# Ending a Strassen-style FFN kernel in two halves of its tokens: the last group's second layer, its norms and its stores

## The chip, the core and the metric

The kernel runs on one core of a Trainium2 chip. The metric is the device time of one execution in microseconds. PE is TensorE (matrix products), DVE is VectorE, ACT is ScalarE, POOL is GpSimd, SP is SyncE, which here only issues DMAs. PSUM is the memory that PE writes to, in banks of 128 partitions by 512 float32 values; SBUF is the working memory.

## The reference

Input x is 4 batches of 512 tokens of 256 features, float32. First a gated scan with its projections, then a feed-forward stack of six blocks, each wrapped in a LayerNorm and a residual:

```python
x = x + _layernorm(_L0_attn_ref(_layernorm(x), ...))
x = x + _layernorm(_L0_ffn_ref(_layernorm(x), ...))

def _L0_ffn_ref(x, W1, B1, W2, B2, LN_G, LN_B):      # N_BLOCKS 6, DIM 256, HIDDEN 1024
    for i in range(N_BLOCKS):
        h = jax.nn.gelu(jnp.einsum('bsd,hd->bsh', x, W1[i]) + B1[i], approximate=False)
        x = jnp.einsum('bsh,dh->bsd', h, W2[i]) + B2[i] + x
        if i < N_BLOCKS - 1:
            x = _layernorm(x, LN_G[i], LN_B[i])
    return x
```

The change concerns the very end: the second product of block 5 for the last two batches, the LayerNorm behind it, the sum with x and the store of the result.

## The kernel before, in words

The four batches form two groups of two (`g` = 0, 1; a group has 1024 tokens). In the feed-forward stack the features lie on the partitions. Both products of a block are done with fewer block products and more sums (a fast matrix multiplication). The first layer (`Hidden`, fed step by step with `take`) makes 1024 hidden features in four `Row`s of 256. `Row.got` applies gelu on ACT and then makes four sums t1 to t4 of hidden blocks: t1 and t3 on DVE (for one row on POOL), t2 and t4 on POOL. These are the tiles `tc`. The second layer (`Output`) has seven parts `p1` to `p7` of four products each, one per row; `p6`, `p5`, `p7`, `p4` read the sums. `partial` takes a PSUM bank, adds the bias and the block's input (DVE, `scalar_tensor_tensor`), `total`, `total11` and `p3` add a second bank (DVE, `tensor_tensor`). Index d is the half of the features, n the batch within the group.

For the last group of the last block, `Output` splits only parts `p5` and `p3` into two columns of 256 tokens; the other five run over 512. Then `finish(u)` does two tiles of 128 tokens: four transposes on PE bring them to a bank with tokens on the partitions, `token_stats` (two DVE instructions per tile) gives mean and variance, `rstd_of` on POOL makes in four small instructions eps added (`ve`), the power −1/2 (`r`), minus the mean (`nm`) and their product (`nb`). ACT adds `nb` to the tile of x, DVE multiplies the bank by `r` and adds, SP issues the store. Two calls follow each half of `p3`: first the tiles of n = 0, then those of n = 1. Other groups have another path through DRAM (`norm`), which ends for the last block in four POOL adds `n<-n,room` and four stores per batch.

The order of instructions on each engine is not that of the program text. `Plan.op` collects every operation with an engine, a cost and its dependencies; `Plan.latest` gives each a due time, counting back from the end of PE's work, and `Plan.run` lets each engine take the one due first of those that are ready by the plan's own costs. An operation that nobody reads (a store) gets as its due time the place that the backward walk over PE has reached (`last[n] = at`).

The end of the program and the line with the due time:

```python
            elif last[n] == 1e9:
                last[n] = at
```

Of the kernel before, what the change touches and what calls it, by code (L numbers as in the profile page):

```python
# [13 lines left out]
ALU = mybir.AluOpType  # L14
PSUM = bass.MemoryType.PSUM

P = 128
LN_EPS = 1e-5
SIGN = {"+": ALU.add, "-": ALU.subtract}
RMS_EPS = 1e-6  # L20
ORDER = "p1 p2 p6 p7 p4 p5 p3".split()
DEFER = 7
HEAD, BY = 2, (2, 1)
POOLROWS = (2,)
WARM = 6
FILL = 2

# [225 lines left out]
class Plan:  # L253
# [31 lines left out]
    def latest(self):  # L285

        last = [1e9] * len(self.ops)
        at = sum(cost for engine, cost, *_ in self.ops if engine == "PE")
        for n in reversed(range(len(self.ops))):
            engine, cost, _, deps, _ = self.ops[n]  # L290
            if engine == "PE":
                at = min(at - cost, last[n])
                last[n] = at
            elif last[n] == 1e9:
                last[n] = at
            for d in deps:
# [51 lines left out]
def kernel(  # L348
# [210 lines left out]
            dst.size * P * 4 / 0.26e6,  # L559
        )  # L560

    def store(dst, src):
        kept = isinstance(dst, View)
        to = dst.ap if kept else dst
        plan.op(
            "SP",
            0.45,
            lambda: nc.sync.dma_start(out=to, in_=src.ap),
            [src],
            [dst] if kept else [],  # L570
            src.size * P * 4 / 0.26e6,
        )
# [461 lines left out]
    class Output:  # L1034


        def __init__(self, i, g, hidden):
            self.i, self.hidden = i, hidden

            n = 2 if (i, g) == (NB - 1, NG - 1) else 1  # L1040
            self.parts = [ts(k, S // n) for k in range(n)]
            w = w2_s
            self.x = xts[g]
            self.left = [(part[:2], int(j)) for part in ORDER for j in part[3:] or "0123"]
            if n == 2:
                half = NP // 2
                self.left = [("p1", j) for j in range(NP)] + [("p2", j) for j in range(NP)]
                self.left += [("p6", j) for j in range(NP)] + [("p5", j) for j in range(half)]
                self.left += [("p7", j) for j in range(NP)]
                self.left += [("p5", j) for j in range(half, NP)] + [("total11", 0)]  # L1050
                self.left += [("p4", j) for j in range(NP)]
# [4 lines left out]
            self.sf, self.s11 = [[None] * 2 for _ in range(ND)], None  # L1056

        def take(self, count=1):
            for part, j in self.left[:count]:
                getattr(self, part)(j)  # L1060
            del self.left[:count]

        def partial(self, d, n):
            s = wide.next()
            stt(s, self.px, b2_s[:, self.i, d : d + 1], self.x[d][n], ALU.add, ALU.add)
            return s

        def total(self, d, n, bank, s):
# [3 lines left out]
        def used(self, j):  # L1072

            self.uses[j] = self.uses.get(j, 0) + 1
            if self.uses[j] == 2:
                hts.back(self.hidden.rows[j].grids[0])

        def done(self, d, n, s):

            self.sf[d][n] = [s[:, ts(t, P)] for t in range(NT)]  # L1080
            if len(self.parts) > 1:
                return
            if n not in self.sent:
                self.sent[n] = rooms.next(), passed.next()
            block, there = self.sent[n]

            part = block[:, ts(d, S)]
            part = part.with_ap(part.ap.rearrange("p (g t r) -> p g t r", g=Q, t=NT))
            blocks_transposed(part, s.ap.rearrange("p (t g c) -> p g t c", t=NT, g=Q), s)
            wide.back(s)  # L1090
            store(there[:, ts(d, S)], block[:, ts(d, S)])
            if all(self.sf[k][n] for k in range(ND)):
                to = self.tokens[n] = rooms.next()
                collected(there, to)
                rooms.back(block)

        def p1(self, j):
            if j == 0:
                self.px = banks.next()
            product(self.px, self.a11[j], self.hidden.rows[j].h[0][0], j == 0)  # L1100
            self.used(j)
            if j == NP - 1:
                self.sn1 = self.partial(0, 0)

        def p2(self, j):
            if j == 0:
                self.py = banks.next()
            product(self.py, self.a12[j], self.hidden.rows[j].h[1][0], j == 0)
            self.used(j)
            if j == NP - 1:  # L1110
                self.total(0, 0, self.py, self.sn1)
                banks.back(self.py)

        def p6(self, j):
            product(self.px, sb2[1][:, j, :], self.hidden.rows[j].sums[1], False)
            tcs.back(self.hidden.rows[j].sums[1])
            if j == NP - 1:
                self.sn2 = self.partial(0, 1)

        def p5(self, j):  # L1120
            if j == 0:
                self.pz = [banks.next()[:, cols] for cols in self.parts]
            for pz, cols in zip(self.pz, self.parts):
                t1 = self.hidden.rows[j].sums[0]
                product(pz, sb2[0][:, j, :], t1[:, cols], j == 0)
            tcs.back(self.hidden.rows[j].sums[0])
            if j == NP - 1 and len(self.parts) == 1 and self.s11:
                self.total11()

        def p7(self, j):  # L1130
            product(self.px, sb2[2][:, j, :], self.hidden.rows[j].sums[2], False)
            if j == NP - 1:
                self.s11 = self.partial(1, 1)
                if len(self.parts) == 1 and " ".join(ORDER).rindex("p5") < " ".join(ORDER).rindex("p7"):
                    self.total11()

        def total11(self, _=None):
            s = self.s11
            for pz, cols in zip(self.pz, self.parts):
                tt("DVE", s[:, cols], pz, s[:, cols], ALU.add)  # L1140
            self.done(1, 1, s)

        def p4(self, j):
            product(self.px, self.a22[j], self.hidden.rows[j].sums[3], False)
            tcs.back(self.hidden.rows[j].sums[3])
            if j == NP - 1:
                s = self.partial(1, 0)
                banks.back(self.px)
# [1 line left out]

        def p3(self, j, part=0):
            pz, cols = self.pz[part], self.parts[part]
            b22 = self.hidden.rows[j].h[1][1]
            product(pz, sb2[3][:, j, :], b22[:, cols], False)
            if part == len(self.parts) - 1:
                hts.back(self.hidden.rows[j].grids[1])
            if j == NP - 1:
                s = wide.next()[:, cols]
                tt("DVE", s, pz, self.sn2[:, cols], ALU.add)
                if len(self.parts) == 1:  # L1160
                    self.done(0, 1, s)
                else:
                    self.sf[0][1] = self.sf[0][1] or []
                    self.sf[0][1] += [s[:, ts(k, P)] for k in range(s.size // P)]
                banks.back(pz)
                if part == len(self.parts) - 1:
                    wide.back(self.sn2)

    class Norm:

# [131 lines left out]
    for i in range(NB):  # L1302
        for g in range(NG):
# [26 lines left out]
            hidden.take(26)  # L1330
            if g == 1 and i + 1 < NB:
                w1_sums(i + 1)
            output = Output(i, g, hidden)
            for u in range(4):
                output.take(2)
                norm.features(u)
            output.take(len(output.left) - DEFER)
            of = (i, g)
    output.take(len(output.left))
    norm = Norm(*of, output)  # L1340
    norm.load_x(0)
    norm.load_x(1)
    for part in range(2):
        for j in range(NP):
            output.p3(j, part)
        norm.finish(2 * part)
        norm.finish(2 * part + 1)
    plan.run()


# [45 lines left out]
```

## Time and profile before

| what | us |
|---|---|
| median of three runs (686.39 to 688.34) | 686.4 |
| the profiled execution | 687.01 |
| its span, from the first to the last instruction | 685.2 |
| PE busy in the span | 671.6 |
| POOL busy in the span | 529.1 |
| DVE busy in the span | 469.2 |
| ACT busy in the span | 358.0 |
| PE's granted clock, mean over the span | 0.996 of full speed |

The times come from one profiled execution; the time of a run is measured around it. In rows of groups, the form `out<-in` names what an instruction writes and reads, then come partitions by elements, the count, the busy time and the mean duration in ns. In the timeline a row has start, duration, engine, line, and what ended the engine's idle time before it. PE rows count two matrix passes for every float32 product, and PEld is the load of its weights, which overlaps other passes. Rows with a q (SPq) are the queue's: they issue DMAs. Nearly all operations are recorded in helpers, so their lines are those of the helper (L502 `tt`, L514 `tscalar`, L524 `stt`, L485 and L487 `act`, L534 `product`, L545 `transpose`, L568 `store`), and groups are told apart by tile names.

### The profile page before, as it was taken

Reading aid. Unit: us, or ns where it says so; the run is one execution under the profiler, and the core shown is the slowest. Engines: PE = TensorE matmul, PEld = TensorE weight load, DVE = VectorE, ACT = ScalarE, POOL = GpSimd, SP = SyncE. Lnnn points to the kernel's source line nnn. Section 1 sums busy time; section 2 is a strip of 40 time slices with the busy share of each in tenths; the row PEclk is TensorE's granted clock in tenths of the full one; section 3 lists DMA queues with packets and bytes.
Section 4 is the critical chain, followed back from the end, with each engine's and each line's share of the span. In section 5 each row is a group of like instructions: output and inputs, shape, how many; then the busy total and the mean of one; then the engine's idle time right before and its main releaser. Section 6 shows DMA issues by size and latency. Waiting matters only on the chain.

```text
span 685.2 us, 8143 instructions
## 1 busy us (share of the span) xinstructions
PE 671.6 (98%) x2328; PEld 436.1 (64%) x2328; DVE 469.2 (68%) x897; ACT 358.0 (52%) x625; POOL 529.1 (77%) x688
## 2 busy tenths in 40 slices
PE   8999999999999999999999999999999999999994
PEld 6565568747658568477476585684774765856853
DVE  5567666866938839759569388397595694783955
ACT  3847757725734636437257346364472573463722
POOL 4997769858988668996589886689965898865763
PEclk9999999999999999999999999999999999999998
DMA  8401312143262142440432622414404206226411
GB/s 254 163 1 62 122 62 80 45 154 92 92 200 77 63 153 53 172 159 17 153 94 73 219 77 76 139 40 178 161 23 154 92 2 225 81 70 190 130 42 63
DMA packets 81837, 73.73 MB, mean 108 GB/s; under 512 B 6272, under 2 KB 70784, under 8 KB 81792
## 3 DMA queue, kind: packets, MB, share of 16 engines
q1 hardware_dynamic: 80960, 72.29, 32.7%
q10 hardware_dynamic: 832, 0.92, 0.4%
q8 instruction: 19, 0.31, 0.2%
q14 instruction: 26, 0.21, 0.1%
HBM read 43.82 MB, written 29.36 MB: 107 GB/s over the span
## 4 chain that ended last, share of the span: by engine, by line
PE 64%; DVE 16%; POOL 8%; ACT 4%; issue 3%; DMA 2%; SPq 0%; DVEq 0%; ACTq 0%; POOLq 0%
PE bank L534 60%; DVE ht L502 9%; POOL tc L502 5%; PE pt L534 4%; DVE tmp L502 2%; DVE st L671 2%; ACT ht L485 2%; DVE tc L502 1%; POOL tx L502 1%; POOL r L502 1%; ACT tmp L487 1%; DMA passed<-room 1%; DMA xt<-in_wk 1%; DVE mv L672 1%; POOL r L514 1%
## 5 line engine op out<-in xcount | busy, mean ns | idle before, releaser
L534 PE MATMUL bank<-tx,sa 128*128 128x256 f32 x672 | 163.1, 381 | 1.7 <-ACT tmp L487 1.5
L487 ACT COPY tmp<-bank 128x512 f32<-128x512 f32 x144 | 83.8, 583 | 137.0 <-PE bank L534 128.2
L534 PEld LDWEIGHTS bank<-tx,sa 128*128 128x128 f32 x672 | 126.4, 190 | 28.3 <-issue 8.2
L502 POOL TENSOR_TENSOR tc<-ht,tc 128x512 f32<-128x512 f32 x96 | 123.6, 1299 | 24.4 <-ACT bank L485 20.6
L485 ACT ACTIVATE ht<-ht,b 128x512 f32<-128x512 f32 x156 | 106.9, 715 | 12.5 <-DVE ht L502 12.5
L502 DVE TENSOR_TENSOR ht<-tmp,bank 128x512 f32<-128x512 f32 x156 | 101.2, 679 | 17.7 <-ACT tmp L487 12.8
L534 PE MATMUL bank<-tc,w 128*128 128x512 f32 x208 | 95.1, 594 | 0.0
L502 DVE TENSOR_TENSOR tmp<-tmp,bank 128x512 f32<-128x512 f32 x96 | 64.4, 677 | 40.2 <-PE bank L534 23.3
L534 PE MATMUL bank<-tc,sb 128*128 128x512 f32 (+1 forms) x200 | 88.2, 581 | 0.9
L534 PE MATMUL bank<-ht,sb 128*128 128x512 f32 (+1 forms) x200 | 88.2, 576 | 0.0
L524 DVE SCALAR_TENSOR_TENSOR tmp<-bank,b,xt 128x512 f32<-128x512 f32 x48 | 35.5, 740 | 76.2 <-PE bank L534 76.2
L534 PE MATMUL bank<-ht,w 128*128 128x512 f32 x192 | 84.4, 593 | 0.0
L502 POOL TENSOR_TENSOR tx<-xt,tx 128x256 f32<-128x256 f32 x108 | 75.8, 734 | 1.0
L485 ACT ACTIVATE n<-x,r 128x256 f32<-128x256 f32 x96 | 50.4, 581 | 37.4 <-POOL r L502 37.4
L534 PEld LDWEIGHTS bank<-tc,sb 128*128 128x128 f32 x200 | 37.2, 190 | 49.6 <-issue 37.9
L534 PEld LDWEIGHTS bank<-tc,w 128*128 128x128 f32 x208 | 39.3, 190 | 40.9 <-issue 37.5
L502 POOL TENSOR_TENSOR tx<-xt 128x256 f32<-128x256 f32 x24 | 17.5, 727 | 60.1 <-ACT xt L485 50.9
L534 PEld LDWEIGHTS bank<-ht,w 128*128 128x128 f32 x192 | 36.5, 190 | 40.7 <-issue 34.9
L502 DVE TENSOR_TENSOR tmp<-bank,tmp 128x512 f32<-128x512 f32 (+1 forms) x54 | 36.0, 666 | 38.2 <-PE bank L534 29.5
L534 PEld LDWEIGHTS bank<-ht,sb 128*128 128x128 f32 x200 | 38.0, 190 | 35.4 <-issue 32.5
L534 PE MATMUL bank<-tx,w 128*128 128x256 f32 x224 | 56.8, 379 | 0.0
L534 PE MATMUL bank<-xt,w 128*128 128x256 f32 x192 | 51.4, 379 | 0.0
(83 smaller groups left out, 1003.6 us busy)
## 6 DMA issues: line engine op xcount, KB each, us to landing
x<-passed SPq DMA_DIRECT2D x120, 128.0 KB, 2.9
passed<-x SPq DMA_DIRECT2D x16, 512.0 KB, 2.7
passed<-x SPq DMA_DIRECT2D x28, 256.0 KB, 2.3
room<-passed SPq DMA_DIRECT2D x56, 128.0 KB, 3.1
w<-in_w1t SPq DMA_DIRECT2D x6, 1024.0 KB, 5.1
w<-in_w2t SPq DMA_DIRECT2D x6, 1024.0 KB, 5.4
passed<-room SPq DMA_DIRECT2D x16, 256.0 KB, 2.1
passed<-room SPq DMA_DIRECT2D x6, 512.0 KB, 2.7
```

The source lines that it names most:

```text
L485: lambda: nc.scalar.activation(dst.ap, src.ap, func, **kw)
L487: else nc.scalar.copy(dst.ap, src.ap),
L502: lambda: on(engine).tensor_tensor(dst.ap, a.ap, b.ap, alu),
L514: lambda: on(engine).tensor_scalar(dst.ap, src.ap, *by, op0, **kw),
L524: lambda: nc.vector.scalar_tensor_tensor(dst.ap, a.ap, by, b.ap, op0, op1),
L534: lambda: nc.tensor.matmul(dst.ap, lhs.ap, rhs.ap, start=start, stop=True, skip_group_check=True),
L671: nc.vector.bn_stats(st.ap, src.ap)
L672: nc.vector.bn_aggr(mv.ap[:, t, :], st.ap)
```

## The change

The last group's `Output` is made twice, over tokens 0 to 255 and 256 to 511, with all seven parts over 256 columns. In the second half `p5` and `p3` are split once more, in two columns of 128 tokens. A half's norms are finished when its parts are there. `finish` now takes the batch, the first tile, how many, and a way:

- POOL (both batches of the first half): ACT computes r·y + nb from the bank, POOL adds x.
- ACT (batch 0 of the second half, two tiles): as before.
- DVE (batch 1 of the second half, one tile at a time): DVE subtracts the mean in the bank, then multiplies by r and adds x; `nm` and `nb` are not made.

In the second half, stores of every other tile go to ACT's DMA queue. The two PSUM buffers `pt` join the pool of banks for this stage. In the plan, operations that nobody reads are due 6 us after PE's end (`AFTER`), for the whole program. The classes hand back hidden tiles only in the last half (`over`), and `add11` takes the place of `total11`.

```diff
+LAST_PARTS = (2 * P, 2 * P)
+LAST_COLUMNS = (P, P)
+LAST_ORDER = "p1 p2 p6 p7 p4 p5".split()
+AFTER = 6.0
+LAST_WAYS = "POOL POOL ACT DVE DVE".split()
...
         at = sum(cost for engine, cost, *_ in self.ops if engine == "PE")
+        end = at + AFTER
...
             elif last[n] == 1e9:
-                last[n] = at
+                last[n] = end
...
-    def store(dst, src):
+    def store(dst, src, engine="SP"):
+        queue = nc.sync if engine == "SP" else nc.scalar
...
-        def finish(self, u):
-
-            pt = banks.next()
-            n, k0 = divmod(2 * u, NT)
-            for k in range(2):
+        def finish(self, n, k0, count, way):
+
+            pt, mv, b = banks.next(), mvs.next(), 2 * self.g + n
+            t0 = self.output.cols.start // P + k0
+            for k in range(count):
                 for d in range(ND):
                     transpose(pt[:, ts(2 * k + d, P)], self.output.sf[d][n][k0 + k])
-            mv, b = mvs.next(), 2 * self.g + n
-            for k in range(2):
-                token_stats(mv, pt[:, ts(k, E)], k)
-            r, nb = rstd_of(mv, rs.next(), lo=0, hi=2)
-            for k in range(2):
-                c, z = k0 + k, nns.next()
-                act(z, self.x[n][:, ts(c, E)], AF.Identity, nb[:, k : k + 1])
-                stt(z, pt[:, ts(k, E)], r[:, k : k + 1], z, ALU.mult, ALU.add)
-                store(out[b, ts(c, P), :], z)
+            y = [pt[:, ts(k, E)] for k in range(count)]
+            for k in range(count):
+                token_stats(mv, y[k], k)
+            if way == "DVE":
+                r = rstd_of(mv, rs.next(), lo=0, hi=count, negative=False)
+                for k in range(count):
+                    tscalar("DVE", y[k], y[k], mv[:, k, 0:1], None, ALU.subtract)
+            else:
+                r, nb = rstd_of(mv, rs.next(), lo=0, hi=count)
+            for k in range(count):
+                c, z = t0 + k, nns.next()
+                x1, rk = self.x[n][:, ts(c, E)], r[:, k : k + 1]
+                if way == "POOL":
+                    act(z, y[k], AF.Identity, nb[:, k : k + 1], rk)
+                    tt("POOL", z, z, x1, ALU.add)
+                elif way == "ACT":
+                    act(z, x1, AF.Identity, nb[:, k : k + 1])
+                    stt(z, y[k], rk, z, ALU.mult, ALU.add)
+                else:
+                    stt(z, y[k], rk, x1, ALU.mult, ALU.add)
+                store(out[b, ts(c, P), :], z, "ACT" if (c + n) % 2 and self.output.over else "SP")
+            banks.back(pt)
...
-    output.take(len(output.left))
-    norm = Norm(*of, output)
-    norm.load_x(0)
-    norm.load_x(1)
-    for part in range(2):
-        for j in range(NP):
-            output.p3(j, part)
-        norm.finish(2 * part)
-        norm.finish(2 * part + 1)
+    x1, at = {}, 0
+    for size in LAST_PARTS:
+        part, at = slice(at, at + size), at + size
+        over = at == S
+        output = Output(i, g, hidden, part, LAST_COLUMNS if over else None)
+        norm = Norm(i, g, output)
+        norm.x = x1
+        if not part.start:
+            for n in range(2):
+                norm.load_x(n)
+            banks.whole.update((id(b), b) for b in pts.bufs)
+            banks.free += pts.bufs
+        output.take(len(output.left))
+        for k in range(0, size // P, 2):
+            norm.finish(0, k, min(2, size // P - k), LAST_WAYS[2 if over else 0])
+        for m, cols in enumerate(output.parts):
+            for j in range(NP):
+                output.p3(j, m)
+            for k in range(cols.start // P, cols.stop // P, 2):
+                way = LAST_WAYS[3 + m if over else 1]
+                norm.finish(1, k, min(2, cols.stop // P - k), way)
```

More of the change, by code (lines that the diff above doesn't have):

```diff
@@ L565, in store @@
         plan.op(
-            "SP",
+            engine,
             0.45,
-            lambda: nc.sync.dma_start(out=to, in_=src.ap),
+            lambda: queue.dma_start(out=to, in_=src.ap),
             [src],
@@ L1034, with __init__ @@
     class Output:
[L1037 to L1041, printed above, removed]
+        def __init__(self, i, g, hidden, cols=slice(0, S), parts=None):
+            self.i, self.hidden, self.cols = i, hidden, cols
+            self.ending = (i, g) == (NB - 1, NG - 1)
+            self.over = cols.stop == S
+            self.parts, at = [], 0
+            for size in parts or (cols.stop - cols.start,):
+                self.parts.append(slice(at, at + size))
+                at += size
             w = w2_s
             self.x = xts[g]
[L1044 to L1051, printed above, removed]
+            order = LAST_ORDER if self.ending else ORDER
+            self.left = [(part[:2], int(j)) for part in order for j in part[3:] or "0123"]
             self.a11 = [w[:, 2 * j, :P] for j in range(NP)]
@@ L1055, in __init__ @@
             self.uses, self.sent, self.tokens = {}, {}, {}
-            self.sf, self.s11 = [[None] * 2 for _ in range(ND)], None
+            self.sf, self.sums11 = [[None] * 2 for _ in range(ND)], 0
         def take(self, count=1):
@@ L1061, in take, with bank, h, t @@
             del self.left[:count]
+        def bank(self):
+            return banks.next()[:, : self.cols.stop - self.cols.start]
+        def h(self, m, n, j):
+            return self.hidden.rows[j].h[m][n][:, self.cols]
+        def t(self, k, j):
+            t = self.hidden.rows[j].sums[k]
+            if self.over and k != 2:
+                tcs.back(t)
+            return t[:, self.cols]
         def partial(self, d, n):
-            s = wide.next()
-            stt(s, self.px, b2_s[:, self.i, d : d + 1], self.x[d][n], ALU.add, ALU.add)
+            s = wide.next()[:, : self.cols.stop - self.cols.start]
+            by = b2_s[:, self.i, d : d + 1]
+            stt(s, self.px, by, self.x[d][n][:, self.cols], ALU.add, ALU.add)
             return s
@@ L1074, in used @@
             self.uses[j] = self.uses.get(j, 0) + 1
-            if self.uses[j] == 2:
+            if self.uses[j] == 2 and self.over:
                 hts.back(self.hidden.rows[j].grids[0])
         def done(self, d, n, s):
-            self.sf[d][n] = [s[:, ts(t, P)] for t in range(NT)]
-            if len(self.parts) > 1:
+            self.sf[d][n] = [s[:, ts(t, P)] for t in range(s.size // P)]
+            if self.ending:
                 return
@@ L1098, in p1 @@
             if j == 0:
-                self.px = banks.next()
-            product(self.px, self.a11[j], self.hidden.rows[j].h[0][0], j == 0)
+                self.px = self.bank()
+            product(self.px, self.a11[j], self.h(0, 0, j), j == 0)
             self.used(j)
@@ L1106, in p2 @@
             if j == 0:
-                self.py = banks.next()
-            product(self.py, self.a12[j], self.hidden.rows[j].h[1][0], j == 0)
+                self.py = self.bank()
+            product(self.py, self.a12[j], self.h(1, 0, j), j == 0)
             self.used(j)
@@ L1114, in p6 @@
         def p6(self, j):
-            product(self.px, sb2[1][:, j, :], self.hidden.rows[j].sums[1], False)
-            tcs.back(self.hidden.rows[j].sums[1])
+            product(self.px, sb2[1][:, j, :], self.t(1, j), False)
             if j == NP - 1:
@@ L1121, in p5, with add11 @@
             if j == 0:
-                self.pz = [banks.next()[:, cols] for cols in self.parts]
+                self.pz = [self.bank()[:, cols] for cols in self.parts]
+            t1 = self.t(0, j)
             for pz, cols in zip(self.pz, self.parts):
-                t1 = self.hidden.rows[j].sums[0]
                 product(pz, sb2[0][:, j, :], t1[:, cols], j == 0)
-            tcs.back(self.hidden.rows[j].sums[0])
-            if j == NP - 1 and len(self.parts) == 1 and self.s11:
-                self.total11()
+            self.add11()
         def p7(self, j):
-            product(self.px, sb2[2][:, j, :], self.hidden.rows[j].sums[2], False)
+            product(self.px, sb2[2][:, j, :], self.t(2, j), False)
             if j == NP - 1:
                 self.s11 = self.partial(1, 1)
[L1134 to L1141, printed above, removed]
+            self.add11()
+        def add11(self):
+            self.sums11 += 1
+            if self.sums11 == 2 * NP:
+                for pz, cols in zip(self.pz, self.parts):
+                    tt("DVE", self.s11[:, cols], pz, self.s11[:, cols], ALU.add)
+                self.done(1, 1, self.s11)
         def p4(self, j):
-            product(self.px, self.a22[j], self.hidden.rows[j].sums[3], False)
-            tcs.back(self.hidden.rows[j].sums[3])
+            product(self.px, self.a22[j], self.t(3, j), False)
             if j == NP - 1:
@@ L1152, in p3 @@
             pz, cols = self.pz[part], self.parts[part]
-            b22 = self.hidden.rows[j].h[1][1]
-            product(pz, sb2[3][:, j, :], b22[:, cols], False)
-            if part == len(self.parts) - 1:
+            product(pz, sb2[3][:, j, :], self.h(1, 1, j)[:, cols], False)
+            done = part == len(self.parts) - 1
+            if done and self.over:
                 hts.back(self.hidden.rows[j].grids[1])
@@ L1159, in p3 @@
                 tt("DVE", s, pz, self.sn2[:, cols], ALU.add)
-                if len(self.parts) == 1:
-                    self.done(0, 1, s)
-                else:
+                banks.back(pz)
+                if done:
+                    wide.back(self.sn2)
+                if self.ending:
                     self.sf[0][1] = self.sf[0][1] or []
                     self.sf[0][1] += [s[:, ts(k, P)] for k in range(s.size // P)]
-                banks.back(pz)
-                if part == len(self.parts) - 1:
-                    wide.back(self.sn2)
+                else:
+                    self.done(0, 1, s)
     class Norm:
@@ L1200, in load_x @@
                 load(self.x[n][:, ts(t, E)], kept[2 * self.g + n][t])
-        def finish(self, u):
-            pt = banks.next()
-            n, k0 = divmod(2 * u, NT)
-            for k in range(2):
+        def finish(self, n, k0, count, way):
+            pt, mv, b = banks.next(), mvs.next(), 2 * self.g + n
+            t0 = self.output.cols.start // P + k0
+            for k in range(count):
                 for d in range(ND):
                     transpose(pt[:, ts(2 * k + d, P)], self.output.sf[d][n][k0 + k])
-            mv, b = mvs.next(), 2 * self.g + n
-            for k in range(2):
-                token_stats(mv, pt[:, ts(k, E)], k)
-            r, nb = rstd_of(mv, rs.next(), lo=0, hi=2)
-            for k in range(2):
-                c, z = k0 + k, nns.next()
-                act(z, self.x[n][:, ts(c, E)], AF.Identity, nb[:, k : k + 1])
-                stt(z, pt[:, ts(k, E)], r[:, k : k + 1], z, ALU.mult, ALU.add)
-                store(out[b, ts(c, P), :], z)
+            y = [pt[:, ts(k, E)] for k in range(count)]
[16 more added lines that the diff above has]
+                    stt(z, y[k], rk, z, ALU.mult, ALU.add)
+                else:
+                    stt(z, y[k], rk, x1, ALU.mult, ALU.add)
+                store(out[b, ts(c, P), :], z, "ACT" if (c + n) % 2 and self.output.over else "SP")
+            banks.back(pt)
         def features(self, u):
@@ L1332 @@
                 w1_sums(i + 1)
+            if (i, g) == (NB - 1, NG - 1):
+                break
             output = Output(i, g, hidden)
```

## The prediction

> **What bounds the kernel now.** I read the page first: engine totals, then the chain, then the last stage by windows, then the last 10 us of the chain piece by piece. The busy line and two stretches:
>
> ```profile
> PE 671.6 (98%) x2328; PEld 436.1 (64%) x2328; DVE 469.2 (68%) x897; ACT 358.0 (52%) x625; POOL 529.1 (77%) x688
> ```
>
> ```profile
> core 0: us, PE busy (x) PEld busy (x) DVE busy (x) ACT busy (x) POOL busy (x), PEclk, DMA share, GB/s
> 650.00:660.00 10.00, 10.00 (x25) 4.53 (x24) 7.34 (x12) 5.92 (x11) 9.85 (x11) 1.00 0.24 83
> 660.00:670.00 10.00, 10.00 (x33) 5.96 (x32) 2.35 (x4) 0.00 (x0) 1.45 (x2) 1.00 0.00 0
> 675.30:685.20 9.90, 1.08 (x8) 0.60 (x6) 5.94 (x18) 3.52 (x8) 4.92 (x15) 0.76 0.31 106
> ```
>
> PE is the bound to 675.3 us, with no gap between 640 and 675 at a granted clock of 1.00. While it works from 660 to 670, DVE, ACT and POOL have almost nothing. Then 9.9 us follow in which PE has only 8 transposes left. Who owns that tail stands in the chain of waits from 640 us on (start, duration, what):
>
> ```profile
> 674.96 0.24 POOL r L514
> 675.27 0.72 POOL r L502
> 677.88 0.82 POOL r L502 x2
> 679.29 0.82 POOL r L502 x2
> 680.72 0.52 ACT n L485
> 681.26 0.88 DVE n L524 x2
> ```
>
> POOL works four `rstd_of` in a row, 674.96 to 680.68: 1.43 us each. Then ACT, two DVE instructions, the last store. It is issued (the timeline below) at 682.19, 0.05 us after DVE ends (681.26 + 0.88 = 682.14), and 3.0 us later the span ends: about 1.8 until the data lands, 1.2 of closing.
>
> Rows for the costs, first from the timeline (start, duration, what), then from the groups by shape (busy us, mean ns | idle before):
>
> ```profile
> 49.08 0.95 PE L534 MATMUL pt<-ones,ht 128*128 128x1 f32 x8
> 672.52 1.04 PE L545 MATMUL bank<-ident,tmp 128*128 128x128 f32 x8
> 673.40 1.89 PE L534 MATMUL bank<-ht,sb 128*128 128x256 f32 x8
> 654.05 7.40 POOL L502 TENSOR_TENSOR tc<-ht,tc 128x512 f32<-128x512 f32 x6
> 650.84 3.24 POOL L502 TENSOR_TENSOR n<-n,room 128x256 f32<-128x256 f32 x4
> 682.19 0.38 SPq L568 DMA_DIRECT2D out<-n  x1
> ```
>
> ```profile
> L534 PEld LDWEIGHTS bank<-tc,w 128*128 128x128 f32 x8 | 1.5, 190 | 1.5 <-issue 1.4
> L502 POOL TENSOR_TENSOR r<-r,neg_half 128x4 f32<-128x4 f32 x33 | 34.2, 1037 | 0.8
> L502 POOL TENSOR_TENSOR r<-r,neg_half 128x2 f32<-128x2 f32 x6 | 4.3, 720 | 0.3
> L502 POOL TENSOR_TENSOR r<-r 128x2 f32<-128x2 f32 x4 | 0.8, 194 | 0.1
> ```
>
> A product is two passes in the trace. Transposes of 128 columns stand (673.40 − 672.52)/8 = 0.110 us apart, passes of 256 columns (675.12 − 673.40)/8 = 0.215 (the next PE row starts at 675.12). So a product costs 0.43 us at 256 columns and 0.86 at 512.
>
> **The change, part by part.** The instruction orders of both kernels agree on every queue until between 630 us (SP) and 644 us (POOL) of this trace. Buffer names differ earlier, no instruction does. So only the end is worked out, on this trace's clock.
>
> *PE, two halves instead of 512 columns.* Before, from 650.18: 20 × 0.859 + 16 × 0.431 + 8 transposes × 0.109 = 24.95, then 0.165 for the last pass to drain: 675.29, as the trace has it. After: 48 products of 256 columns, 48 × 0.431 = 20.69; 16 of 128 columns × 0.22 = 3.52; now 14 of the 16 transposes stand ahead of the last product, 1.53. Sum 25.74, the last product ends at 676.08: **0.79 later**. The first 0.6 of this is transposes that were in the tail.
>
> The 128-column product is new. Here the trace and a rule are to be weighed. The row says that a weight load lasts 190 ns; were passes to follow at that pace, 32 of them would cost 32 × (0.190 − 0.110) = 2.6 us more. The Trainium skill, "TensorE: Matmul & The Clock Gate", section on LDWEIGHTS, gives columns / 1.2 GHz, 107 ns for 128, however few columns are streamed; so narrow products win nothing below that, but pay no 190. The passes with one column start between 49.08 and 49.89 (the next PE row), 0.10 us apart: the rule holds, 190 ns is latency. Bounds 0.215 and 0.38 per product; I take 0.22.
>
> *PE's waits.* The halves ask for the hidden rows sooner: 12 products of 256 columns stand ahead of the first that reads POOL's second `tc`, so it is due at 650.18 + 12 × 0.431 = 655.35. In this trace that `tc` is done at 656.56 (654.05 + 2 × 1.23 + 0.05). The new due time of operations that nothing reads (six us past PE's end) moves what held POOL behind these six `tc`: the four steps of `r` for the last tile set (1.7 us in all) and the four adds of the 650.84 row (3.24), with ACT's four normalizations (0.59 each) and one pair of DVE statistics (0.6). POOL can then start the `tc` when DVE and ACT deliver, up to 2 us sooner. Worked queue by queue, the second `tc` is ready about 0.6 ahead of its product, the other waits 0.4 to 1.1 ahead. PE runs in order, so all products behind a waiting one, and with them every norm, would slip by the wait. Bounds: 0, and 656.56 − 655.35 = 1.2 if POOL gains nothing. I take 0.
> What is moved back is not late elsewhere: the adds and their four stores on SP come at about 661 to 664 instead of 651 to 654, under PE's products, and the kernel ends 20 us later. SP also issues one x load ahead of four gathers, 0.45 us later for these; they feed the statistics moved back. The order of stores on SP stays.
>
> *First half's norms.* Two `rstd_of` (1.43 each), four POOL adds (0.73 each), four ACT instructions reading PSUM (nearest row 0.59 each), four statistics pairs (0.62 each), four stores. They fall between 666 and 675 us. What hides them is the second half's 12 us of products; POOL is done at about 674.7, 1.8 us before it is needed. Without that cover they'd cost POOL 5.8 us in the tail. Cost: nothing.
>
> *The tail.* Three norms remain: the two tiles of n = 0 together (way ACT), then n = 1 in two single tiles (way DVE). Statistics of the two tiles need the four transposes after p4; DVE ends them at about 676.5. From there POOL again: one `rstd_of` of 1.43; two short ones that leave out nm and nb: 0.23 for eps, 0.56 for pow on one element, 0.04 of gaps, 0.83 each. The one-element pow stands in no row: a line through 1.037 (four) and 0.720 (two) gives 0.56; below it can't be less than a plain operation on r, 0.194; above, 0.72. It counts twice on the chain: −0.7 to +0.3. So POOL ends at 676.5 + 0.1 + 1.43 + 1.66 = 679.65. DVE then has three SCALAR_TENSOR_TENSOR in its order, because the single tiles stand ahead of the ready pair: 0.03 + 0.40 + 0.40 + 0.48 = 1.31, to 680.96. The two subtractions of the mean in PSUM (nearest row of DVE's TENSOR_SCALAR at 128x256: 0.40 each) lie under POOL's pow; without it, 0.8.
>
> *Stores on two queues.* The Trainium skill, "Trainium Kernel Development and Optimization", Key Constraints, speaks against a gain: queues share the 16 DMA engines, and a second one "only saves the sequencer's issue time". The trace agrees: the last store left 0.05 after its data. SP issues 0.43 to 0.47 apart against DVE's 0.40, so SP alone would be 0.1 late after three stores. By the rule 0 to −0.1; a queue that halved the transfer would give −0.8. A store on ACT's queue stands behind ACT's last two instructions, done by then. I take the same 3.05 from the last DVE end to the span's end.
>
> **Sum:** 680.96 + 3.05 = 684.0 us of span against 685.2, −1.2: the tail shrinks from 9.91 to 7.93, and 0.79 goes to PE. The profiled execution took 687.01, 1.8 above its span; 1.2 off gives 685.8 for it. The median of the runs is 686.4, 0.6 below the profiled one, so **685.2**.
>
> **Rivals.**
> - *PE waits for the hidden rows.* For: POOL is 98% busy from 650 to 660 and PE was already released by `tc` at 656.6. Against: 5 us of POOL work leaves that stretch. Price up to 1.2, which eats the gain: 686.4.
> - *Faster.* The one-element pow costs as little as a plain operation: −0.7, 684.5, and if the second queue also gains half of the 0.8 named above, 684.1, or all of it, 683.7. For: no row shows the fixed part of a pow, the line through two sizes only infers 0.40. Against: just that line, and the 0.05 of the last store's issue.
> - *Slower than before: narrow products at the pace of 190 ns.* Place: the 16 products of p5 and p3 in the second half. Price 2.6, so 687.8. It beats the gain once a pass takes over 0.11 + 1.2/32 = 0.15 us. Against: the 0.10 and 0.11 spacing above.
> - *The second queue does nothing.* Probable, and already in the sum.
>
> **Chances.** Forecast case 0.63 (684.5 to 685.9), faster 0.18 (683.7 to 684.5), waits 0.14 (685.9 to 686.7), narrow products 0.05. The bound of 0.3% is 2.06 us, about what a measurement of this kernel can tell from no change: under 684.3 is faster, over 688.5 slower. The faster case lies mostly under 684.3, and the forecast's low edge adds a little: 0.18 faster; of the slow case, and only if its pace goes with a wait, 0.03 slower; 0.79 within. The range 683.8 to 686.8 takes in pow's lower bound with most of a faster store, and the full wait; outside are the narrow products and the edges of the others.
>
> **What would show it.** Right: PE's last product ends near 676.1 with 128-column passes 0.11 apart and no PE gap from 650 on; POOL's pow on one element near 0.56; three `rstd_of` in POOL from 676.5 to 679.7; the last store issued near 681.0. Wrong: a wait of PE for `tc` near 655, passes 0.15 apart or more, a chain of the end that no longer runs through POOL, or a store from ACT's queue that lands over 2 us after its issue.

## The result, and the profile after

| | before | changed |
|---|---|---|
| median of 21 runs | 687.13 us (686.03 to 688.76) | 685.47 us (684.70 to 686.52) |
| the profiled execution | 687.01 | 685.20 |
| its span | 685.2 | 683.4 |

The changed kernel takes 0.9978 of the time before, with a 95% interval of 0.9971 to 0.9984: about 1.5 us less, between 1.1 and 2.0 (the two medians differ by 1.66). That is under the 0.3% which the prediction set as its bound. The first three runs of before had a median of 686.4; 21 runs put it at 687.1, so the times on both sides lie higher than the prediction's, and the difference is what counts.

Read first the busy line and three stretches of the changed kernel (columns as before: length, PE, PEld, DVE, ACT, POOL, PEclk, DMA share, GB/s):

```profile
PE 671.9 (98%) x2384; PEld 443.6 (65%) x2384; DVE 469.7 (69%) x902; ACT 357.8 (52%) x623; POOL 531.9 (78%) x692
```

```profile
650.00:660.00 10.00, 10.00 (x49) 8.70 (x48) 7.28 (x14) 3.89 (x6) 7.80 (x9) 1.00 0.00 1
660.00:670.00 10.00, 10.00 (x55) 8.87 (x54) 4.73 (x14) 2.80 (x6) 4.96 (x12) 1.00 0.16 54
675.83:683.40 7.57, 0.44 (x2) 0.20 (x2) 4.14 (x13) 0.91 (x2) 2.88 (x8) 0.86 0.20 69
```

The totals tell almost nothing. The stretches do: PE stays full from 650 to 670 at a granted clock of 1.00, POOL has fallen from 9.85 to 7.80 in the first of them, and DVE, ACT and POOL, which had 2.35, 0.00 and 1.45 from 660 to 670 before, now have 4.73, 2.80 and 4.96 there. Two things fill that stretch. One is the four POOL adds that the later due time moved back, with the ACT instructions ahead of them. The other is the first half's norms, whose last adds on POOL end at 674.42 (673.01 + 1.41), ahead of the end of PE's last product at 675.83. The timeline of POOL has both:

```profile
661.11 2.79 POOL L508 TENSOR_TENSOR n<-n,room 128x256 f32<-128x256 f32 x4 [0.71 <-ACT n L491]
673.01 1.41 POOL L508 TENSOR_TENSOR n<-n,x 128x256 f32<-128x256 f32 x2 [0.67 <-ACT n L491]
```

Behind PE's last product POOL has 2.88 instead of 4.92 and ACT 0.91 instead of 3.52.

The chain of waits of the changed kernel at the end (start, duration, what):

```profile
676.92 0.49 DVE bank L520
...
677.78 0.19 DVE mv L679
677.98 0.02 issue
678.00 0.50 DVE bank L520
678.50 0.06 issue
678.57 0.23 POOL r L520
...
679.50 0.48 DVE n L530
```

Before, this chain stood on POOL from 674.96 to 680.68. The list now stands on DVE up to 678.50 and goes to POOL for the last eps and pow only. But a list of this kind shows one releaser at each step. The timeline of POOL in the same stretch:

```profile
676.25 0.22 POOL L520 TENSOR_SCALAR r<-mv 128x2 f32<-128x2 f32 x1 [1.82 <-DVE mv L679]
676.55 0.71 POOL L508 TENSOR_TENSOR r<-r,neg_half 128x2 f32<-128x2 f32 x1
677.25 0.54 POOL L520 TENSOR_SCALAR r<-mv 128x1 f32<-128x1 f32 x2
677.75 0.57 POOL L508 TENSOR_TENSOR r<-r,neg_half 128x1 f32<-128x1 f32 x1
678.29 0.20 POOL L508 TENSOR_TENSOR r<-r 128x2 f32<-128x2 f32 x1
678.57 0.23 POOL L520 TENSOR_SCALAR r<-mv 128x1 f32<-128x1 f32 x1
678.88 0.58 POOL L508 TENSOR_TENSOR r<-r,neg_half 128x1 f32<-128x1 f32 x1
```

POOL works its three `rstd_of` from 676.25 to 679.46 and is never idle for more than 0.09 us. What its instruction at 678.57 reads, the mean and variance of the last tile (`mv`), was ready at 677.97, while POOL was on earlier work until 678.49. DVE's second subtraction ended at 678.49 too, so the list could go either way at this point. The instruction at 678.57 follows POOL's own one by 0.08 us, as that at 676.55 does, so POOL would have started no sooner without the subtraction. So POOL still owns the tail. DVE comes close behind: in the 5.79 us from 674.98 to its last end it is busy for 4.96, and it waits 0.62 us for POOL's last pow.

Since all profiles differ in where the last second layer begins (649.5 to 651.3 us), I measure from its first product. In the traces:

| us from the first product of the last second layer | before | changed |
|---|---|---|
| to the end of PE's last product | 25.11 | 25.99 |
| from there to the last DVE end | 6.85 | 4.93 |
| from there to the landing of the last store | 1.81 | 1.81 |
| sum to the landing | 33.77 | 32.74 |
| the span after the landing | 1.28 | 0.84 |

### The profile page after: what moved, and what is told of

The parts are those of the page before. It is cut to its first block, busy times and chain, and to the rows that moved or that the text cites. A ratio compares the mean times of both kernels' runs of the same rounds, so it can differ in the third digit from the quotient of the medians.

```text
span 683.4 us, 8266 instructions
## 1 busy us (share of the span) xinstructions
PE 671.9 (98%) x2384; PEld 443.6 (65%) x2384; DVE 469.7 (69%) x902; ACT 357.8 (52%) x623; POOL 531.9 (78%) x692
## 4 chain that ended last, share of the span: by engine, by line
PE 66%; DVE 17%; POOL 8%; ACT 4%; issue 4%; DMA 0%; DVEq 0%; POOLq 0%; ACTq 0%
PE bank L540 60%; DVE ht L508 9%; POOL tc L508 5%; PE pt L540 5%; DVE tmp L508 3%; DVE st L678 2%; ACT ht L491 2%; DVE tc L508 1%; ACT tmp L493 1%; POOL tx L508 1%; DVE mv L679 1%; POOL r L508 1%; POOL r L520 1%; ACT bank L491 0%; DMA x<-in_x 0%
## 5 line engine op out<-in xcount | busy, mean ns | idle before, releaser
L540 PE MATMUL bank<-tc,w 128*128 128x512 f32 (+1 forms) x216 | 95.2, 578 | 0.0
L540 PE MATMUL bank<-tc,sb 128*128 128x512 f32 (+2 forms) x208 | 88.2, 560 | 0.9
L540 PE MATMUL bank<-ht,sb 128*128 128x512 f32 (+2 forms) x208 | 88.0, 555 | 0.0
L530 DVE SCALAR_TENSOR_TENSOR tmp<-bank,b,xt 128x512 f32<-128x512 f32 (+1 forms) x52 | 36.4, 700 | 74.7 <-PE bank L540 74.7
L540 PE MATMUL bank<-ht,w 128*128 128x512 f32 (+1 forms) x200 | 83.0, 567 | 0.0
L540 PEld LDWEIGHTS bank<-tc,w 128*128 128x128 f32 x216 | 40.7, 190 | 39.9 <-issue 36.1
L540 PEld LDWEIGHTS bank<-ht,w 128*128 128x128 f32 x200 | 37.9, 190 | 38.1 <-issue 31.8
L491 ACT ACTIVATE n<-x,r 128x256 f32<-128x256 f32 x90 | 47.7, 587 | 26.7 <-POOL r L508 26.7
L508 DVE TENSOR_TENSOR tmp<-bank,tmp 128x512 f32<-128x512 f32 (+2 forms) x54 | 35.4, 655 | 36.1 <-PE bank L540 27.4
```

The source lines that it names most:

```text
L491: lambda: nc.scalar.activation(dst.ap, src.ap, func, **kw)
L508: lambda: on(engine).tensor_tensor(dst.ap, a.ap, b.ap, alu),
L530: lambda: nc.vector.scalar_tensor_tensor(dst.ap, a.ap, by, b.ap, op0, op1),
L540: lambda: nc.tensor.matmul(dst.ap, lhs.ap, rhs.ap, start=start, stop=True, skip_group_check=True),
```

## The experiments

"To the landing" is the sum above, one profile each. Times are medians, and the ratios are taken against runs of before on the same chip. The medians of before beside the later kernels were 687.16 (one part to one queue), 687.03 (one column and the first mean on ACT) and 687.35 (the two repeats).

| kernel | to the landing, us | median, us | ratio to before (95%) |
|---|---|---|---|
| before | 33.77 | 687.13 | |
| changed | 32.74 | 685.47 | 0.9978 (0.9971 to 0.9984) |
| one part | 34.39 | 687.63 | 1.0007 (0.9999 to 1.0015) |
| way ACT | 34.13 | 686.93 | 0.9994 (0.9986 to 1.0003) |
| due times as before | 32.93 | 685.45 | 0.9977 (0.9967 to 0.9987) |
| one queue | 32.85 | 685.56 | 0.9977 (0.9968 to 0.9986) |
| one column | 32.57 | 685.37 | 0.9975 (0.9964 to 0.9986) |
| mean on ACT | 31.67 | 684.80 | 0.9967 (0.9954 to 0.9980) |
| changed, again | 32.74 | 685.32 | 0.9974 (0.9964 to 0.9984) |
| mean on ACT, again | 31.68 | 684.77 | 0.9962 (0.9949 to 0.9975) |

**One part: the halves taken back, the new ways kept.**

```diff
-LAST_PARTS = (2 * P, 2 * P)
-LAST_COLUMNS = (P, P)
+LAST_PARTS = (4 * P,)
+LAST_COLUMNS = (2 * P, 2 * P)
```

> The changed kernel without its halves: all seven parts over 512 tokens again (p5 and p3 in two columns of 256 as before), but norms by the new ways (two joined tiles each, ways ACT and DVE), new due times, two queues. Measure: from the first product of the last second layer to the landing of the last store; 33.8 us in the kernel before, 32.7 in the changed one. Theory (the halves carry the gain, because they put four of the eight norms under PE's products; the ways alone leave POOL four rstd_of in the tail): 34.1 us, the time back at that of the kernel before or 0.3 above it (+1.4 us against the changed kernel). Rival (the ways carry it: fewer steps on POOL in the tail are what pays): 32.7 to 33.2, +0 to +0.5 us. PE's last product some 25.1 us after the first instead of 26.0 either way.

Measured: 34.39 us, PE's last product 25.12 after the first. The gain is gone and 0.6 more is lost. The windows row of this kernel from its first statistics of the tail to the last DVE end:

```profile
673.97:683.82 9.85, 3.55 (x21) 2.76 (x19) 9.56 (x30) 1.70 (x4) 4.42 (x12) 0.79 0.17 58
```

DVE is busy for 9.56 of 9.85 us, POOL for 4.42. Eight tiles end here, and four of them have their subtraction on DVE. The theory had the direction and a little too small a loss: it counted POOL's steps, and DVE had become the bound. This kernel keeps the changed one's order of parts and the two added banks, and PE takes the time of before (25.11); so these two alone don't move PE.

**Way ACT: the halves kept, the single tiles normed as before.**

```diff
-LAST_WAYS = "POOL POOL ACT DVE DVE".split()
+LAST_WAYS = "POOL POOL ACT ACT ACT".split()
```

> The changed kernel with the way ACT for all four tiles of the second half (so the two single tiles get nm and nb on POOL and an instruction on ACT again, and no subtraction on DVE). Theory (POOL owns the tail, the two short rstd_of save it 2 x 0.47 us, and DVE's subtractions lie under POOL's pow): POOL ends 0.9 us later, DVE 1.1 us later, 33.9 us from the first product to the last landing against 32.7, +1.1 us in time. Rival (DVE is as full as POOL in the tail, so its two subtractions of 0.49 us cost what POOL saves): +0 to +0.3 us.

Measured: 34.13 us, 1.39 more than the changed kernel, and 1.46 in the medians, which were not taken side by side. Of the 1.39, 1.14 lie behind PE's last product, as the theory said (1.1); 0.21 lie ahead of it, where a weight load waits for a hidden row of DVE's, and 0.05 in the last store. The rival, with at most 0.3, falls. The timeline of this kernel at the end:

```profile
681.13 1.70 ACT L491 ACTIVATE n<-x,r 128x256 f32<-128x256 f32 x4 [6.29 <-POOL r L508]
681.24 0.33 POOL L508 TENSOR_TENSOR r<-r 128x1 f32<-128x1 f32 x2
681.67 1.68 DVE L530 SCALAR_TENSOR_TENSOR n<-bank,r,n 128x256 f32<-128x256 f32 x4 [2.70 <-ACT n L491]
```

POOL works three whole `rstd_of` (to 681.57), ACT waits for it, and DVE stands idle for 2.70 us before its four last instructions. In the changed kernel DVE waits 0.62. With the run above this makes nearly a square: both kernels keep the new due times and the second queue, and this one keeps the way POOL for the first half. To the landing neither halves nor ways gain alone (+0.36 and +0.62 against before); together they gain 1.03. With halves and the old ways, PE's last product comes 1.09 us later than before, and the tail behind it is only 0.78 shorter, because three whole `rstd_of` stand on POOL in place of four and all four DVE instructions come after them. New ways without halves fill DVE with eight tiles.

**Due times as before.**

```diff
-                last[n] = end
+                last[n] = at
```

> The changed kernel with the due times of the kernel before for operations that nobody reads; everything else as changed. Theory of the prediction (the later due time is what frees POOL in time for the hidden sums that the halves read sooner): POOL works the four steps of r and the four adds ahead of its last sums again, PE waits 0.6 to 1.2 us for a tc near 655, and every later product with it: +0.6 to +1.2 us. Rival (the order of PE's products, which the planner makes from the same costs, goes round the late sums by itself; a replay queue by queue gives waits of 0.2 us in all): -0.1 to +0.3 us.

Measured: 32.93 us, +0.19, and no difference in the medians (685.45 and 685.47). The prediction's reason falls. The timeline of POOL in this kernel, then of PE, then of PE in the changed kernel:

```profile
654.62 6.18 POOL L508 TENSOR_TENSOR tc<-ht,tc 128x512 f32<-128x512 f32 x5
```

```profile
656.48 0.81 PE L540 MATMUL bank<-tc,sb 128*128 128x256 f32 x3
```

```profile
655.02 1.24 PE L540 MATMUL bank<-tc,sb 128*128 128x256 f32 x5
```

POOL is as late here as it was before: five sums in one block from 654.62, the adds ahead of them. But PE does not wait for them: the planner, which counts that the sums come late, has put products of the second half that need no sum in front, so the first reader starts at 656.48 instead of 655.02. The waits of PE ahead of its last product, in the list of waits of this kernel from 649 us on, are for a hidden row and for a bank of DVE's:

```profile
PEld bank L540 <- DVE ht L508: 0.4, 1, 0.4
PEld bank L540 <- DVE tmp L530: 0.3, 1, 0.3
```

With them PE's last product comes 26.57 us after the first instead of 25.99. Of these 0.58 us only 0.19 reach the landing, since the tail behind is 0.36 shorter in this order.

**One queue.**

```diff
-store(out[b, ts(c, P), :], z, "ACT" if (c + n) % 2 and self.output.over else "SP")
+store(out[b, ts(c, P), :], z, "SP")
```

> The changed kernel with all stores on SP. Theory (the second queue saves only issue time): SP issues 0.43 to 0.47 apart against DVE's 0.40, so the last store leaves 0.1 to 0.2 us later, landing 1.78 us after its issue as before: +0.1 to +0.2 us in the trace, no difference in time that can be measured. Rival (two queues also shorten the transfer): the last landing comes 2.2 us or more after its issue, +0.4 to +0.8 us.

Measured: 32.85 us, +0.11. The last store is issued 0.14 us after DVE's last end instead of 0.03, and lands 1.78 us after its issue, as in the changed kernel. This is what the theory said, and the rival's longer landing is not there.

**One column: no products of 128 columns.**

```diff
-LAST_COLUMNS = (P, P)
+LAST_COLUMNS = (2 * P,)
```

> The changed kernel with the second half's p5 and p3 in one column of 256 tokens: no 128-column products, and the two tiles of n = 1 joined in one rstd_of (way DVE). Measure: from the first product of the last second layer to the landing of the last store, 32.7 us in the changed kernel. Theory (passes of 128 columns cost what their columns cost, so PE changes by less than 0.1 us; POOL has two joined rstd_of instead of one joined and two single, 0.6 us less work; but both tiles' statistics now wait for the whole of p3): PE's last product 0.25 us earlier because more transposes stand behind it, the landing 0.3 us earlier, 32.4. Rival (the early statistics of the first single tile are worth more than POOL's saving, because DVE is full in the tail too): 0.2 to 0.6 us later, 32.9 to 33.3.

Measured: 32.57 us, 0.17 less than the changed kernel; PE's last product 0.33 earlier. The sign is the theory's, the size is half, and the gain is PE's alone: the part from PE's last product to the last DVE end is 0.11 longer, and the last store lands 0.07 later after it. POOL's saving of 0.6 us shortened nothing, because DVE is next: its two subtractions of 0.49 us stand in a row ahead of its four last instructions, which then follow without a wait. In time nothing can be told.

**Mean on ACT: a version that takes from POOL and DVE at once.**

```diff
-LAST_WAYS = "POOL POOL ACT DVE DVE".split()
+LAST_WAYS = "POOL POOL MEAN MEAN MEAN".split()
...
+            if way == "MEAN":
+                q = rs.next()
+                ve, r = (q[:, k, 0:count] for k in range(2))
+                nm = rs.next()[:, 2, 0:count]
+                tscalar("DVE", ve, mv[:, 0:count, 1], LN_EPS, None, ALU.add)
+                tscalar("DVE", nm, mv[:, 0:count, 0], -1.0, None, ALU.mult)
+                tt("POOL", r, ve, neg_half[:, 0:count], ALU.pow)
...
+                elif way == "MEAN":
+                    act(z, y[k], AF.Identity, nm[:, k : k + 1])
+                    stt(z, z, rk, x1, ALU.mult, ALU.add)
```

> The changed kernel with another way for all four tiles of the second half: DVE adds eps and negates the mean (two instructions of 1 or 2 elements), ACT subtracts the mean from the bank while POOL makes the pow, POOL does nothing but the pow, and DVE's one SCALAR_TENSOR_TENSOR multiplies by r and adds x. POOL loses 7 of its 10 instructions behind the last product, DVE its two subtractions of 0.49 us against six small ones. Theory (POOL's chain and DVE's work bound the tail together, so only taking from both shortens it): POOL's last pow ends near 679.1 and DVE near 679.6 on the clock where the changed kernel has 679.6 and 680.9; landing 1.3 us earlier, 31.4 us from the first product, about -1.3 us in time against the changed kernel, 0.9957 to 0.9962 of the kernel before. Rival A (DVE's small instructions and ACT's three extra semaphores eat it): -0.0 to -0.4 us. Rival B (what was left is PE's transposes behind the last product): no change.

Measured: 31.67 us, 1.07 less than the changed kernel, and the fastest of all. The groups of this kernel from 677 us on, and the windows row of its tail:

```profile
L530 DVE SCALAR_TENSOR_TENSOR n<-n,r,x 128x256 f32<-128x256 f32 x4 | 1.7, 481 | 0.0
L491 ACT ACTIVATE n<-bank,r 128x256 f32<-128x256 f32 x4 | 1.6, 475 | 3.8 <-DVE r L520 3.8
L508 POOL TENSOR_TENSOR r<-r,neg_half 128x1 f32<-128x1 f32 x2 | 1.2, 597 | 0.0
L508 POOL TENSOR_TENSOR r<-r,neg_half 128x2 f32<-128x2 f32 x1 | 0.7, 716 | 2.6 <-DVE r L520 2.6
```

```profile
675.59:680.26 4.67, 1.29 (x10) 0.86 (x8) 4.42 (x19) 1.57 (x4) 1.84 (x3) 1.00 0.16 54
```

DVE's idle time before its last four instructions is 0.0. It is busy for 4.42 of 4.67 us (in the changed kernel 4.96 of 5.79), POOL for 1.84 (2.88). So it is now DVE that bounds the tail. Counted from the first product, POOL's last pow ends 0.59 us earlier than in the changed kernel (the theory had 0.5) and DVE 1.12 earlier (the theory had 1.3). What is missing, 0.2 us, is therefore on DVE, which has little free time left. POOL's first pow waits 2.6 us for its eps, which stands on DVE behind a later tile's statistics, but POOL is no longer the bound.

**Before once more, and the other two once more.** No edit; three profiles to separate the change from the scatter of one execution.

> The kernel before, unchanged, profiled once more. The first profile of before shows 33.77 us from the first product of the last second layer to the last landing, 650.18 us ahead of it and 1.28 us behind it; the changed kernel 32.74, 649.84 and 0.84. Theory (only the middle part is the change's; what lies ahead of it and behind it is scatter of one execution): the middle repeats within 0.1 us, the other two do not. Rival (the change also moves the start or the end of the program): 650.2 and 1.3 again.

> The changed kernel, unchanged, profiled and timed once more, beside the kernel with the mean on ACT. Theory: 32.7 us in the middle part within 0.1, the time ahead of it anywhere between 649.5 and 651.3 as in the other profiles; 0.9976 to 0.9980 of the kernel before. Rival (start and end belong to the change): 649.8 and 0.84 again.

> The kernel with the mean on ACT once more, on the same chip as the changed kernel. If its 1.07 us in the trace are real in time, it is 0.7 to 1.3 us below the changed kernel here; if they are lost again (a store or the closing takes them), less than 0.3 us.

Measured: the sum to the landing repeats to 0.01 us: 33.78, 32.74, 31.68. The part ahead of it does not: the last second layer of the changed kernel began at 649.84, then at 650.80. Most of these 0.96 us arise at the start; the same instruction of PE in the first and the second profile of the changed kernel:

```profile
7.96 0.60 PE L540 MATMUL bank<-tx,xt 128*128 128x256 f32 x2
```

```profile
8.79 0.70 PE L540 MATMUL bank<-tx,xt 128*128 128x256 f32 x2 [0.99 <-DMA xt<-in_wk]
```

PE waits 0.99 us for the load of a weight tile in the second and not at all in the first; it is 0.92 behind from there on. It is not always the start: in the kernel of one part and in the first profile with the mean on ACT, 0.8 to 1.0 us more come at 389 us, where PE waits 0.8 and 0.7 us for a sum on POOL. The second profile with the mean on ACT has no such delay, so this too is scatter. The part behind the landing, however, repeats: 1.28 and 1.28 in before, 0.84 and 0.84 in the changed kernel. So of these two sides the theory was right on one and the rival on the other: the span's last 0.44 us belong to the change. In the trace POOL's sequencer starts its closing DRAIN 0.36 us after its last semaphore in before, and 0.07 after it in the changed kernel, and that DRAIN lasts 0.22 and 0.08; together this is the 0.44. Why is open; none of the runs touches it. It isn't the last store, which lands 1.76 and 1.78 us after its issue.

The mean on ACT is 0.55 us faster than the changed kernel on the same chip (medians 684.77 and 685.32). That is less than the 1.06 of the trace and lies between the two outcomes named (0.7 to 1.3, and less than 0.3); the medians of 6 and 9 runs, which scatter by over a microsecond, don't settle the rest.

## Why the prediction was right

- **The sum.** Forecast: −1.2 us to the landing. Measured: −1.03 there, and 0.44 more behind it that was not forecast. The predicted 685.2 for the median stands against 685.47, with a base that had turned out 0.7 higher. That the median came so close is partly luck: the higher base and a gain larger than forecast (1.66 between the medians, against 1.2) work against each other. The mechanism is judged by the terms below.
- **PE, +0.79.** Measured +0.88. Products of 128 columns cost what the spacing said, to 0.0025 us a pass, which over 32 passes makes 0.08 of the missing 0.09: in the changed kernel eight passes take 0.90 us, from 673.33 to the next PE row.

```profile
673.33 1.06 PE L540 MATMUL pt<-ht,sb 128*128 128x128 f32 x8
674.23 0.39 PE L540 MATMUL bank<-ht,sb 128*128 128x128 f32 x2
```

That is 0.1125 us for one, against the 0.190 of the weight-load row; the rival of slow narrow products fell. The Trainium skill, "TensorE: Matmul & The Clock Gate", section on LDWEIGHTS, gives columns / 1.2 GHz for a load, by which 128 columns are estimated at 107 ns; the pace lies near that. Whether the load or the 128 columns that stream sets it can't be told from these rows; the 190 ns do not.
- **PE's waits, 0.** Right in size. The step's reason was wrong: "the new due time … moves what held POOL" is true of POOL, as the 9.85 that became 7.80 show, but PE did not need it. With the old due times PE's order goes round the late sums, and 0.19 us is the whole difference at the landing. The slack was also smaller than the 0.6 given: the `tc` that PE waits for first was done at 654.71 (the first of the three in POOL's row), 0.31 ahead of its product at 655.02 and only 0.09 ahead of that product's weight load at 654.80:

```profile
653.43 3.85 POOL L508 TENSOR_TENSOR tc<-ht,tc 128x512 f32<-128x512 f32 x3 [1.89 <-ACT bank L491]
```

```profile
654.80 0.19 PEld L540 LDWEIGHTS bank<-tc,sb 128*128 128x128 f32 x1
```

- **The tail, from 6.85 to 4.88 us behind PE's last product.** Measured 4.93. Piece by piece: statistics of the pair ready at 676.16 (forecast 676.5 on a clock that ran 0.34 later, the same); POOL from there 3.30 instead of 3.15 (the forecast's own terms, 0.1 + 1.43 + 1.66, make 3.19, not 3.15); DVE from POOL's end 1.30 against 1.31. The one-element pow, which no row had shown, took 0.572 against the 0.56 read off the line through two and four elements:

```profile
L508 POOL TENSOR_TENSOR r<-r,neg_half 128x1 f32<-128x1 f32 x2 | 1.1, 572 | 0.1
L520 DVE TENSOR_SCALAR bank<-bank,mv 128x256 f32<-128x256 f32 x2 | 1.0, 493 | 0.1
```

- **The subtractions, "under POOL's pow".** Right, with a size that was off: 0.493 each in PSUM instead of 0.40. The second ended at 678.49, when POOL came free for the last set, whose mean had been there since 677.97; so they kept POOL from nothing. But they use up cover: only 0.62 us of DVE's time is left idle. The prediction named "a chain of the end that no longer runs through POOL" as a sign against it. The list of the chain looks like that sign, and POOL's timeline, without a gap from 676.25 to 679.46, shows that it has not come.
- **The second queue, 0 to −0.1.** Measured −0.11. The rule of the Trainium skill, "Trainium Kernel Development and Optimization", Key Constraints, that only issue time is saved, agrees with the run on one queue (issue 0.14 us after the data instead of 0.03, landing 1.78 us after the issue in both).
- **Closing.** Taken as the same 1.2 us; it was 0.44 shorter. This is the one term that the sum had wrong without a reason in view.

## What to carry to other kernels

When a tail is bound by one engine's chain, cut the work that reaches it (here by halves under the matrix engine's cover) and look at the same time which engine is next: to the landing, halves alone and other norms alone lost, and both together gained. The next microsecond of the trace came only when work moved from both of the full engines to the idle third one. Before a chain of waits is believed, read the timeline of the engine that it leaves: here that engine had no free time. A due time in a planner that sees late operands need not be what keeps the matrix engine fed; take it back before crediting it. For changes of 0.2%, compare stretches between two fixed instructions of the trace: they repeat to 0.01 us where the whole span scatters by more than one.

## What the runs showed of the hardware that I had not expected

- DVE's TENSOR_SCALAR in place in PSUM, 128x256, takes 493 ns, more than its SCALAR_TENSOR_TENSOR from PSUM and SBUF (479 and 476 ns); one on 1 or 2 elements takes 150 ns.
- The end of the program after the last landing is not constant: 1.28 us in before, 1.13 in the kernel of one part, 0.84 or 0.85 in all others, twice the same where a kernel was profiled twice.
- The last second layer began between 649.55 and 651.31 us in eleven profiles. Where this was followed up, PE had waited 0.99 us for a weight load in the first 9 us, or 0.7 to 0.8 us for a sum on POOL at 389 us.
